# Four reads of transposed tokens moved up by one write in SyncE's queue

## The chip, the cores and the metric

The kernel runs on one core of a Trainium2 chip. The metric is device time in microseconds (us), from the start of the program to its end. An engine executes its own instructions in the order in which the program lists them; engines and transfers tell each other by semaphores.

## What is computed

There are 64 graphs of 256 tokens with 512 channels, in float32, and an adjacency matrix of 256 x 256 for each. Two layers follow each other. Cut to what matters:

```
# layer 0: gated attention, 8 heads of 64 channels
h    = relu(layernorm(x))
q, k, v = h @ Wq.T, h @ Wk.T, h @ Wv.T
attn = softmax(where(adj, q k^T / 8, -inf))        # per head
c    = attn @ v
gate = sigmoid(concat(c, h) @ Wg.T + bg)
x    = x + gate * h + (1 - gate) * c
# layer 1: graph attention, one head
h    = relu(layernorm(x))
Wh   = h @ W
e    = leaky_relu(Wh a1 + (Wh a2)^T, 0.2), masked by adj
x    = x + elu(softmax(e) @ Wh)
```

All matrix products are float32 on TensorE (PE). Each of the larger ones is split into quarters and computed with seven block products instead of eight (Strassen), so it needs sums of input blocks, made on GpSimd (POOL), and sums of partial results, made on VectorE (DVE).

## The kernel before

**Rounds.** The work is software-pipelined. `emit_round(i)` (L650) emits one round, and a round works on four graphs at different stages: graph i (attention), p = i + 1 (its first products and scores), q = i - 1 (gate, then the second layernorm) and r = i - 2, o = i - 3 (graph attention and output). Rounds -1 to 66 are emitted one after the other. The order on every engine is that of the calls, written out by hand; no scheduler changes it.

**Transposes.** Three kinds of matrices must be transposed between stages: the normalized tokens h, the probabilities e, and the gated result y. Apart from the first two graphs and the last ones this is done in three steps: DVE transposes blocks of 32 x 32 (`a_turn`, `turn`, `g_turn`), SyncE (SP) issues a write of the blocks to a scratch tensor in DRAM (`a_send`, `p_send`, `g_send`), and SP issues four reads that bring them back in the other order (`a_fetch`, `p_fetch`, `g_fetch`), each for 32 of the 128 partitions.

**SP's queue.** SP issues nearly all the transfers. It takes them in order; where one has to wait for a semaphore, all that are behind it wait too. From the start of round i the order is

```
p_send(p)      x4   L248  write h of graph p
a_send(i,0,0)  x1   L392  first write of probabilities
a_send(i,0,1)  x1   L392
a_send(i,1,0)  x1   L392  third write
a_send(i,1,1)  x1   L392  fourth write
p_fetch(p)     x4   L255  read h of graph p transposed into hT
a_fetch(i,0,0) x4   L397  read the first probabilities back
g_send(q)      x1   L392  write y
a_fetch(i,0,1) x4   L397
g_fetch(q)     x4   L397  read y back (yT)
a_fetch(i,1,0) x4   L397
g_store(o)     x1   L640  output
g_send_e(r)    x4   L248
load_graph     x2   L92, L93  next x and adj
a_fetch(i,1,1) x4   L397
g_fetch_e(r)   x4   L255
g_send_h(q)    x4   L248,  later g_fetch_h(q) x4 L255
```

A write of probabilities can be issued when `a_turn` (L386, DVE) of its two halves is done. In the program `a_turn(i,1,1,0)`, `g_diff(q)` (POOL, L456), the gate steps "2 c00 4 c10" (PE and DVE/ACT), `g_tanh` (ACT) and `a_turn(i,1,1,1)` stand between the third and the fourth write.

**Semaphores of transfers.** SP's transfers take eight semaphores in turn. In the trace a transfer waits for the one that used the same semaphore eight transfers before, besides its data and its buffer.

**Who uses hT.** The tile `hT` (three buffers) holds the transposed tokens of graph p. `p_sums` (L152 to L155 by way of `token_sums`) makes four sums of its quarters on POOL, S_l. The product of q and k, `p_qk`, starts with step "1", `pma_qk`, which reads hT alone. In PE's order it comes straight after the last step of `g_wh` ("3", `pmc_wh`). Two block columns later PE transposes the edge column of `wh` (`g_edges`, `pe`, L556), and then step "6" of `p_qk`, `pmb_qk`, needs the second sum (L153).

**DVE beside it.** While PE computes `g_wh`, DVE adds up its partial results (L185) and mixes the gate: `g_mix` (L469 and L471, each with two inputs in SBUF), then `g_turn` (L487), whose result `g_send` writes.

Of the kernel before, what the change touches and what calls it, by code (L numbers as in the profile page):

```python
# [22 lines left out]
def kernel(  # L23
# [626 lines left out]
    def emit_round(i):  # L650


        p, q, r, o = i + 1, i - 1, i - 2, i - 3

        def do(fn, g, *args):
            if 0 <= g < B:
                fn(g, *args)
# [37 lines left out]
        do(a_turn, i, 1, 0, 0)  # L695
        do(a_turn, i, 1, 0, 1)
        do(a_send, i, 1, 0)
        do(a_turn, i, 1, 1, 0)
        do(g_diff, q)
        run(g_gate, q, "2 c00 4 c10")  # L700
        do(g_tanh, q, 0)
        do(a_turn, i, 1, 1, 1)
        do(a_send, i, 1, 1)
        do(p_fetch, p)
        do(p_mask, p)
        chore(chores, 2)
        run(g_gate, q, "3 c01")
# [106 lines left out]
    with tc.manual_schedule(engines={getattr(mybir.EngineType, e) for e in ("PE", "SP", "Pool", "DVE", "Activation")}):  # L814
        load_graph(0)
        load_weight("q", nc.sync)
        load_weight("k", nc.scalar)
        load_weight("v", nc.sync)
        p_stats(0, 0)
        p_stats(0, 1)  # L820
        for fn in (p_root, p_bias, p_norm, p_transpose_pe):
            fn(0)
        for i in range(-1, B + 3):
            emit_round(i)
            graphs.pop(i - 3, None)
# [32 lines left out]
```

## Time and profile before

| | |
|---|---|
| device time, median of 3 runs | 3191.97 us (3191.17 to 3193.47) |
| the profiled execution's own time | 3185.72 us |
| its span, first to last instruction | 3183.9 us |
| PE busy | 3125.0 us, 98% of the span |
| DVE, POOL, ACT busy | 2467.8, 1506.3, 1413.6 us |
| SP's transfers, share of 16 DMA engines | 73.9% |
| mean granted clock of PE | 0.994 |

The profiled execution is 6.25 us shorter than the median of the other runs; durations below are its own. The number in front of a line of the timeline is the start in us from the beginning of the span, the next is the length. Idle time is put in brackets with what ended it. A line can join several instructions of one kind (x4), and its length then includes what stands between them.

### The profile page before, as it was taken

Reading aid. Unit: us, or ns where it says so; the run is one execution under the profiler, and the core shown is the slowest. Engines: PE = TensorE matmul, PEld = TensorE weight load, DVE = VectorE, ACT = ScalarE, POOL = GpSimd, SP = SyncE. Lnnn points to the kernel's source line nnn. Section 1 sums busy time; section 2 is a strip of 40 time slices with the busy share of each in tenths; the row PEclk is TensorE's granted clock in tenths of the full one; section 3 lists DMA queues with packets and bytes.
Section 4 is the critical chain, followed back from the end, with each engine's and each line's share of the span. In section 5 each row is a group of like instructions: output and inputs, shape, how many; then the busy total and the mean of one; then the engine's idle time right before and its main releaser. Section 6 shows DMA issues by size and latency. Waiting matters only on the chain.

```text
span 3183.9 us, 66670 instructions
## 1 busy us (share of the span) xinstructions
PE 3125.0 (98%) x22716; PEld 2723.9 (86%) x22716; DVE 2467.8 (78%) x6366; ACT 1413.6 (44%) x3976; POOL 1506.3 (47%) x2183
## 2 busy tenths in 40 slices
PE   7899999999999999999999999999999999999997
PEld 6888888888889888888888898888888888888984
DVE  6777877877877878778778778778787787787774
ACT  2343543543544534435435445445344344454442
POOL 2454544544544545535445445445454454454453
PEclk9999999999999999999999999999999999999998
DMA  5678778777777777787787777777877877877761
GB/s 169 176 173 204 189 180 206 185 180 206 182 190 199 184 191 195 180 203 187 178 211 184 181 207 182 190 197 177 200 189 182 205 186 179 211 183 183 204 170 44
DMA packets 1103394, 590.63 MB, mean 186 GB/s; under 512 B 685776, under 2 KB 1029328, under 8 KB 1103056
## 3 DMA queue, kind: packets, MB, share of 16 engines
q1 hardware_dynamic: 1102000, 585.32, 73.9%
q8 instruction: 182, 2.98, 0.4%
q14 instruction: 156, 1.28, 0.1%
q10 hardware_dynamic: 1056, 1.05, 0.1%
HBM read 304.88 MB, written 281.28 MB: 184 GB/s over the span
## 4 chain that ended last, share of the span: by engine, by line
PE 90%; DVE 4%; POOL 2%; DMA 2%; issue 1%; SPq 1%; ACT 0%; DVEq 0%; POOLq 0%; ACTq 0%
PE pmb_qk L174 11%; PE pmb_z L174 9%; PE pc L418 7%; PE pma_qk L174 7%; PE pmc_qk L174 7%; PE ps L338 6%; PE po L615 6%; PE pma_z L174 6%; PE pmc_z L174 6%; PE pmb_v L174 5%; PE pmb_wh L174 5%; PE pma_v L174 3%; PE pmc_v L174 3%; PE pmc_wh L174 3%; PE pma_wh L174 3%; DVE e L353 1%
## 5 line engine op out<-in xcount | busy, mean ns | idle before, releaser
L362 ACT ACTIVATE e<-e,low 128x256 f32<-128x256 f32 x1024 | 506.5, 499 | 63.3 <-DVE low L353 63.3
L204 POOL TENSOR_TENSOR rs_l<-ve_l,mhalf 128x2 f32<-128x2 f32 x128 | 89.0, 695 | 869.7 <-DVE ve_l L200 869.7
L353 DVE CUSTOM_DVE_ANT_0 e<-ps,mask 128x256 f32<-128x256 f32 x1024 | 362.1, 415 | 100.1 <-PE ps L338 100.1
L377 POOL TENSOR_SCALAR e<-e,rec 128x256 f32<-128x256 f32 x768 | 352.7, 477 | 148.8 <-DVE rec L370 100.4
L386 DVE STREAM_TRANSPOSE eb<-e 128x512 f32<-128x512 f32 x512 | 351.8, 696 | 76.7 <-POOL e L377 63.4
L213 ACT ACTIVATE h_l<-x,nb_l,rs_l 128x512 f32<-128x512 f32 x256 | 194.1, 805 | 212.4 <-DVE nb_l L208 123.5
L152 POOL TENSOR_TENSOR S_l<-hT_l 128x256 f32<-128x256 f32 x128 | 93.4, 730 | 395.9 <-DMA hT_l<-there_h 361.9
L637 POOL TENSOR_TENSOR x<-x,pos 128x512 f32<-128x512 f32 x128 | 160.1, 1272 | 229.3 <-DVE pos L633 229.3
L615 PE MATMUL po<-wh,egT 128*128 128x512 f32 x512 | 242.5, 617 | 2.1 <-ACT egT L598 2.1
L338 PE MATMUL ps<-qk 64*128 64x256 f32 x2048 | 238.9, 383 | 0.6 <-DVE v L185 0.6
L418 PE MATMUL pc<-eT,v 128*64 128x256 f32 x2048 | 235.9, 382 | 0.1
L338 PEld LDWEIGHTS ps<-qk 64*128 64x128 f32 x2048 | 193.1, 187 | 45.3 <-DVE ve_l L200 21.9
L418 PEld LDWEIGHTS pc<-eT,v 128*64 128x64 f32 x2048 | 141.3, 137 | 86.7 <-DMA eT<-there_e 16.3
L239 DVE STREAM_TRANSPOSE h_l<-h_l 128x512 f32<-128x512 f32 x248 | 167.8, 695 | 54.7 <-ACT h_l L213 54.7
L615 PEld LDWEIGHTS po<-wh,egT 128*128 128x128 f32 x512 | 94.3, 194 | 118.5 <-issue 95.1
L362 ACT ACTIVATION_READ_ACCUMULATOR e<-e,low 128x1 f32 x1024 | 194.8, 190 | 0.0
L196 DVE BATCH_NORM_STATS2 bs_l<-x 128x6 f32<-128x512 f32 x256 | 172.9, 675 | 5.4 <-DMA x<-in_x_dram 5.4
L461 ACT ACTIVATE z<-z,hbg 128x256 f32<-128x256 f32 x256 | 116.1, 502 | 105.9 <-DVE z L185 105.9
L456 POOL TENSOR_TENSOR d<-hT_l,cT 128x512 f32<-128x512 f32 x128 | 160.5, 1274 | 0.0
L428 ACT COPY cT<-pc 128x512 f32<-128x512 f32 x128 | 74.9, 585 | 184.5 <-PE pc L418 184.5
L174 PEld LDWEIGHTS pma_z<-hT_l,wgh_sb 128*128 128x128 f32 x1024 | 129.2, 192 | 30.4 <-issue 30.4
L174 PE MATMUL pma_qk<-hT_l,wq_sb 128*128 128x128 f32 x1024 | 139.6, 280 | 11.9 <-DMA hT_l<-there_h 10.1
(146 smaller groups left out, 7964.8 us busy)
## 6 DMA issues: line engine op xcount, KB each, us to landing
there_e<-eb SPq DMA_DIRECT2D x256, 512.0 KB, 3.4
eT<-there_e SPq DMA_DIRECT2D x1024, 128.0 KB, 3.9
there_h<-h_l SPq DMA_DIRECT2D x496, 128.0 KB, 3.3
hT_l<-there_h SPq DMA_DIRECT2D x496, 128.0 KB, 3.3
x<-in_x_dram SPq DMA_DIRECT2D x64, 512.0 KB, 4.0
out_dram<-x SPq DMA_DIRECT2D x64, 512.0 KB, 4.2
there_y<-y SPq DMA_DIRECT2D x62, 512.0 KB, 3.3
yT<-there_y SPq DMA_DIRECT2D x248, 128.0 KB, 3.4
```

What stands on the lines that cost most here:

```text
L174: nc.tensor.matmul(bank[key][(slice(None), *cols)], lhsT, rhs, start=first and i == 0, stop=last and i == len(todo) - 1, skip_group_check= ...
L196: nc.vector.bn_stats(bs, s["x"][:, t, :])
L213: nc.scalar.activation(h[:, t, :], s["x"][:, t, :], AF.Relu, bias=s["nb"][:, t:t + 1], scale=s["rs"][:, t:t + 1])
L239: nc.vector.transpose(h[:, t, :], h[:, t, :])
L338: nc.tensor.matmul(psc[jj, i][:, t, :], qk[r:r + DK, 0, jj, t * P:(t + 1) * P], qk[r:r + DK, 1, jj, :], start=True, stop=True,)
L353: nc.vector.tensor_tensor_reduce(s["e", half, jj][:, i, t, :], s["ps", half][jj, i][:, t, :], s["mask"][:, t, :], -SCALE, HUGE, ALU.add, A ...
L362: nc.scalar.activation(e, e, AF.Exp, bias=s["low", half][:, jj, i, t:t + 1], scale=-1.0, accum_out=s["sums", half][:, jj, i, t:t + 1],)
L377: nc.gpsimd.tensor_scalar(e, e, rec[:, i, t:t + 1], 1.0, ALU.mult, ALU.mult)
L386: nc.vector.transpose(s["eb", half, jj][:, :, 4 * i:4 * i + 4, :].rearrange("p b n c -> p n b c"), e)
L418: nc.tensor.matmul(pc[i * DK:(i + 1) * DK, jj, :].rearrange("p (t a c) -> p t a c", t=NT, c=32), s["v"][:, kc, hd * DK:(hd + 1) * DK], eT[ ...
L456: nc.gpsimd.tensor_tensor(d, s["hT"][:, :, js, :], s["cT"][:, :, js, :], ALU.subtract)
L615: nc.tensor.matmul(pm, s["egT"][:, t, kc, :], s["wh"][:, kc, :, :HH], start=(kc == 0), stop=(kc == NT - 1))
```

## The change

The call `do(p_fetch, p)` moves up by eight lines. Its four reads are now issued behind the third write of probabilities and ahead of the fourth. No instruction is added or removed, and no other engine's order changes: `p_fetch` issues on SP alone. The fourth write comes four transfers later in SP's queue, and the use of the eight semaphores turns with it.

```diff
         do(a_turn, i, 1, 0, 0)
         do(a_turn, i, 1, 0, 1)
         do(a_send, i, 1, 0)
+        do(p_fetch, p)
         do(a_turn, i, 1, 1, 0)
         do(g_diff, q)
         run(g_gate, q, "2 c00 4 c10")
         do(g_tanh, q, 0)
         do(a_turn, i, 1, 1, 1)
         do(a_send, i, 1, 1)
-        do(p_fetch, p)
         do(p_mask, p)
         chore(chores, 2)
         run(g_gate, q, "3 c01")
```

## The prediction

> **What bounds the kernel now.** I read the page from the top: the busy shares, then the groups of instructions with their idle time, then the waits, and last the timeline of a round.
>
> ```profile
> PE 3125.0 (98%) x22716; PEld 2723.9 (86%) x22716; DVE 2467.8 (78%) x6366; ACT 1413.6 (44%) x3976; POOL 1506.3 (47%) x2183
> ...
> L152 POOL TENSOR_TENSOR S_l<-hT_l 128x256 f32<-128x256 f32 x128 | 93.4, 730 | 395.9 <-DMA hT_l<-there_h 361.9
> ...
> L174 PE MATMUL pma_qk<-hT_l,wq_sb 128*128 128x128 f32 x1024 | 139.6, 280 | 11.9 <-DMA hT_l<-there_h 10.1
> ```
>
> PE has 59 us of idle time in all, so no change of order can be worth more than 2%. POOL waits 361.9 us for the tile that the moved reads fill, which looks like much, but POOL is idle half of the time and PE works meanwhile. What counts is the last row: PE itself waited 10.1 us for hT. That is the size of the prize, give or take.
>
> Next, round by round. In an undisturbed round of the timeline the blocks of PE follow each other without a gap:
>
> ```profile
> 1651.03 1.03 PE L174 MATMUL pmc_wh<-w_sb,S_l 128*128 128x257 f32 x4
> ...
> 1651.81 0.73 POOL L152 TENSOR_TENSOR S_l<-hT_l 128x256 f32<-128x256 f32 x1 [6.08 <-DMA hT_l<-there_h]
> ...
> 1651.90 1.05 PE L174 MATMUL pma_qk<-hT_l,wq_sb 128*128 128x128 f32 x8
> ```
>
> The last read landed at 1651.56 (the trace's record of single transfers), POOL started 0.25 us after it, and PE, which needs the same tile, started 0.34 us after it. So hT lands just when PE wants it: such a round takes 48.29 us and loses nothing, but there is no margin. When a transfer is late, PE waits:
>
> ```profile
> 1116.82 1.03 PE L174 MATMUL pmc_wh<-w_sb,S_l 128*128 128x257 f32 x4
> 1118.26 1.13 PE L174 MATMUL pma_qk<-hT_l,wq_sb 128*128 128x128 f32 x8 [0.41 <-DMA hT_l<-there_h]
> ...
> 99.62 2.05 PE L174 MATMUL pma_qk<-hT_l,wq_sb 128*128 128x128 f32 x8 [6.00 <-DMA hT_l<-there_h]
> ```
>
> Here 1.44 us lie between two starts instead of the usual 0.87. The second example is the first round that reads hT through DRAM, still among the start-up work.
>
> **What the Trainium skill says.** "DMA: Bandwidth & Descriptors", Anatomy of one DMA, says that a wait for a semaphore happens on the issuing sequencer and that DMA engines just consume their queues; the section on queues, rings and completion order adds that descriptors are consumed in ring order on each engine. The trace agrees: while the fourth write waits for DVE, SP issues nothing, although hT's source landed 2.4 us (median) before the third write was out. "SBUF — State Buffer", Who interferes with whom, says that a DVE instruction with two inputs in SBUF and a GpSimd instruction that reads SBUF exclude each other. The trace agrees: the output's sum `pos` takes 0.68 us alone and 1.19 us where POOL's sums run beside it, and POOL's L154 takes 1.18 instead of 0.73 us.
>
> **The change, part by part.**
>
> ```profile
> 1645.76 0.32 SPq L392 DMA_DIRECT2D there_e<-eb  x1
> 1646.25 2.61 SPq L255 DMA_DIRECT2D hT_l<-there_h  x4
> 1648.97 1.95 SPq L397 DMA_DIRECT2D eT<-there_e  x4
> ```
>
> *The four reads.* The third write is issued at 1644.02 and takes SP 0.32 us. SP then waits until 1645.76 for the last `a_turn`, issues the fourth write, and starts the reads at 1646.25. With the change they start at 1644.34 + 0.10 = 1644.44, 1.81 us earlier; this is the median over all rounds too. Their data has landed and the buffer is long free, so they bring no new wait. From issue to landing they took 3.3 us just behind a write; the same holds behind the third, so I keep it (2.6 us is the shortest seen for such reads). hT lands at 1651.56 - 1.81 = 1649.75.
>
> *The fourth write.* It is ready at 1645.76, but SP is busy with the reads until 1644.44 + 2.66 = 1647.1: 1.3 us later. Its data is read back by the last `a_fetch` from 1665.49 on, so about 15 us cover a landing of some 3.3 us. Its source buffer is next needed in the following scores, over 25 us later. Cost: nothing.
>
> *What is behind on SP.* The first `a_fetch` moves from 1648.97 to about 1647.5. The waiting time of SP was filled with the reads, so everything behind is earlier or equal, up to `g_send`, which waits for DVE at 1652.34 as before. The eight semaphores: one of the first `a_fetch` reads now waits for the first hT read (landed by about 1647.7, needed at about 1649.0), and the fourth write for a write of h that landed by 1641.8. No wait comes of it.
>
> *PE, steady rounds.* I measured from the last `pmc_wh` matmul to the first `pma_qk` in the 61 rounds from 149 us on. The usual distance is 0.22 us; 17 rounds lie over 0.25, and the excess adds up to 6.8 us, the largest 1.17. All of them are below the 1.81 us gained. After a wait the first block also takes about 0.08 us longer (1.13 for 1.05), in all 1.9 us. Both go: 8.7 us.
>
> *PE, first round.* At 99.62 the shift is 2.5 us, since the fourth write is later there. PE starts at about 97.1, and DVE, 5.6 us idle ahead of the first sum of `p_qk`, can follow: 2.5 us. The matmuls there ran at half clock (2.05 us for 1.05), and whether the clock returns earlier or later is open: plus or minus 1.5 us.
>
> *POOL and DVE, the new collision.* The sums now run from about 1649.95 instead of 1651.81. In an undisturbed round DVE's second L471 starts at 1650.30, with two inputs in SBUF; today POOL is idle then. It must wait for L152 to end at about 1650.68 and needs some 0.54 us more (as `pos` does), so it ends at about 1651.2 instead of 1650.98: 0.2 us, at worst 0.5 as seen on `pos`. L487 and two L185 follow, and their last result is needed by `pe` on PE. From its end to `pe` there are 0.72 us, of which some 0.15 are the weight load and the signal; 0.55 us of cover. Cost: nothing, up to small change in odd rounds. `g_send` may be 0.2 us later, but the reads queued in front of y are gone earlier.
>
> *What is late next.* The last probabilities: the matmul that first needs them starts 1.0 us (median) after they land, at worst 0.14 us. I allow 0.7 us for rounds that meet this instead.
>
> Sum: 6.8 + 1.9 + 2.5 - 0.7 = 10.5 us. The profiled execution would fall from 3185.7 to 3175.2. The runs' median stands 6.3 us above that execution, and I apply the same difference to it: 3191.97 - 10.5 = 3181.5. Bounds of the cost: from 3 us (only the larger waits go, and half comes back at the next one) to 17 us (if the 6.3 us that the runs have over the profile are also late hT, which no view here shows).
>
> **The rivals.**
>
> *It is hidden anyway.* Late rounds might owe their delay to something that moves with PE, so that the next wait, the last probabilities (0.14 us at worst), takes most of it back. For it: 44 of 61 rounds lose nothing today. Against it: that wait costs about 1 us in all rounds together. The gain would be 0 to 6 us: 3186 to 3192, within what can be told.
>
> *Slower, through the lock between POOL and DVE.* If L471 loses twice, to L152 and to L153, it ends about 1.1 us late, against 0.55 us of cover; PE then stalls 0.55 us in each of about 60 rounds: 33 us, 3225 us. It decides from 0.55 us of delay on. For it: L208, 0.15 us long alone, takes 0.72 beside POOL's sums, so the delays are real and can reach 0.57. Against it: on `pos` DVE got its turn after one instruction of POOL in all 60 rounds.
>
> *The change doesn't do what it says.* The reads could be held at the new place, if h's write were late. It landed at least 0.47 us before the third write was issued, in every round. This is part of the first rival.
>
> **How the numbers follow.** Forecast (gain 6.5 to 17 us) 0.70, hidden 0.22, slower by the lock or another way 0.08. About 0.2%, 6.4 us, is what a measurement can tell from no change, so these are also the chances of faster, within, slower. The range 3174 to 3190 holds the forecast from its largest gain and most of the hidden case; the slower tail is left out.
>
> **What would show it.** Right: PE's wait for hT falls from 10.1 us to below 4, nearly all of it in the first round; POOL's L152 waits about 1.8 us less per round (361.9 to about 250); L255 is issued in front of the last `there_e`; L471 takes about 0.9 us in most rounds. Wrong: `pe` or `pmb_qk` waits for DVE's `wh` for more than 10 us, or waits for eT grow by as much as those for hT fall, or hT's time to landing rises by more than 1 us.

## The result and the profile after

| | median, us | runs |
|---|---|---|
| before | 3191.57 (3190.14 to 3193.47) | 6 |
| changed | 3178.28 (3176.11 to 3178.95) | 6 |

The changed kernel is 13.3 us faster: ratio 0.9957, 95% interval 0.9945 to 0.9970. The forecast was 3181.5 us. In two more comparisons the ratio was 0.9947 (0.9935 to 0.9960) and 0.9948 (0.9936 to 0.9961). The profiled execution took 3178.95 us, its span 3177.2 us.

The page of the changed kernel, and the group of the first `p_qk` block from its list of groups:

```profile
PE 3122.1 (98%) x22716; PEld 2726.9 (86%) x22716; DVE 2481.4 (78%) x6366; ACT 1414.0 (45%) x3976; POOL 1528.5 (48%) x2183
...
L152 POOL TENSOR_TENSOR S_l<-hT_l 128x256 f32<-128x256 f32 x128 | 95.2, 744 | 276.6 <-DMA hT_l<-there_h 240.0
```
```profile
L174 PE MATMUL pma_qk<-hT_l,wq_sb 128*128 128x128 f32 x1024 | 137.7, 278 | 5.0 <-DMA hT_l<-there_h 3.6 <-DVE hT_l L143 1.4
```

PE's wait for hT fell from 10.1 to 3.6 us, and those 3.6 us are one wait, in the first round that reads hT (6.00 us before). POOL's wait fell by 122 us, nearly all of it time in which PE was at work.

SP's queue of the changed kernel, in a round of the middle:

```profile
1638.67 0.32 SPq L392 DMA_DIRECT2D there_e<-eb  x1
1639.17 2.60 SPq L255 DMA_DIRECT2D hT_l<-there_h  x4
1641.82 0.60 SPq L392 DMA_DIRECT2D there_e<-eb  x1
```

The reads follow the third write 0.50 us after its issue and fill the time in which SP used to wait for DVE. hT now lands 2.15 us ahead of PE's start of `pma_qk` (median) instead of 0.29 us. The timeline of the same round, POOL, DVE and PE:

```profile
1644.55 0.73 POOL L152 TENSOR_TENSOR S_l<-hT_l 128x256 f32<-128x256 f32 x1 [4.17 <-DMA hT_l<-there_h]
...
1644.93 0.89 DVE L471 SCALAR_TENSOR_TENSOR z<-d,cT 128x512 f32<-128x512 f32 x1
...
1645.35 1.06 POOL L153 TENSOR_TENSOR S_l<-S_l,hT_l 128x256 f32<-128x256 f32 x1
...
1646.53 1.05 PE L174 MATMUL pma_qk<-hT_l,wq_sb 128*128 128x128 f32 x8
...
1648.31 0.38 PE L556 MATMUL pe<-ident,wh 128*128 128x128 f32 x2
```

In the undisturbed round of the kernel before that the prediction shows, the same two instructions were

```profile
1650.30 0.68 DVE L471 SCALAR_TENSOR_TENSOR z<-d,cT 128x512 f32<-128x512 f32 x1
...
1652.61 0.73 POOL L153 TENSOR_TENSOR S_l<-S_l,hT_l 128x256 f32<-128x256 f32 x1
```

The collision is there: L471 takes 0.89 us instead of 0.68, L153 1.06 instead of 0.73. PE's `pe` starts on time. What is late instead, elsewhere in the same execution, is the last part of the probabilities. In the worst round PE waits almost 1 us in the middle of `pc`:

```profile
456.32 2.81 PE L418 MATMUL pc<-eT,v 128*64 128x256 f32 x24
460.08 1.08 PE L418 MATMUL pc<-eT,v 128*64 128x256 f32 x8 [0.95 <-DMA eT<-there_e]
```

Below, the rounds from 149 us on, in which PE's blocks have one order, are called steady: `p_qk` starts 61 times there, with 60 whole rounds between. "Excess" is what a round, or a stretch of it between two blocks of PE, takes over its usual (tenth percentile) length, summed over the rounds; it includes what a restart costs after a wait. The "lateness of hT" is the excess from the start of the last `wh` matmul to the first of `pma_qk`, as in the prediction, and the "eT excess" is that of the stretch of `pc`.

### The profile page after: what moved, and what is told of

Read it like the earlier page. It is cut to its first block, busy times and chain, and to the rows that moved or that the text cites. A ratio compares the mean times of both kernels' runs of the same rounds, so it can differ in the third digit from the quotient of the medians.

```text
span 3177.2 us, 66671 instructions
## 1 busy us (share of the span) xinstructions
PE 3122.1 (98%) x22716; PEld 2726.9 (86%) x22716; DVE 2481.4 (78%) x6366; ACT 1414.0 (45%) x3976; POOL 1528.5 (48%) x2183
## 4 chain that ended last, share of the span: by engine, by line
PE 94%; DMA 2%; DVE 2%; issue 1%; POOL 1%; SPq 0%; ACT 0%; POOLq 0%; DVEq 0%; ACTq 0%
PE pmb_z L174 11%; PE pmb_qk L174 10%; PE po L615 7%; PE ps L338 7%; PE pma_z L174 7%; PE pmc_z L174 7%; PE pc L418 7%; PE pma_qk L174 7%; PE pmc_qk L174 7%; PE pmb_wh L174 5%; PE pmb_v L174 5%; PE pmc_wh L174 3%; PE pma_wh L174 3%; PE pma_v L174 3%; PE pmc_v L174 3%; DMA eT<-there_e 1%
## 5 line engine op out<-in xcount | busy, mean ns | idle before, releaser
L187 ACT COPY qk<-pma_qk 128x512 f32<-128x512 f32 x64 | 37.5, 585 | 245.5 <-PE pma_qk L174 245.5
```

## The experiments

**Theory.** The loss was PE waiting for late hT; margin above the largest lateness is worth nothing. **Rivals.** The gain comes from SP's queue as a whole (every later read comes earlier), or it is small and the profile caught a good execution. Kernels of one comparison ran on one chip, beside the kernel before.

**1. The kernel before, profiled again, twice.** No edit.

> The kernel before, for a second profile: the first one was 6.3 us shorter than the median of its runs. Theory (the runs have more late hT than the profile caught): an execution near 3192 to 3195 us shows 12 to 15 us of excess at the step from wh to pma_qk in the 60 steady rounds and the start-up together, instead of 6.8 and 6.2. Rival (the difference lies in the start-up or in the clock): the steady rounds show 10 to 11 us as before, and the difference is found elsewhere.

> The same once more, with the same expectations, so that two executions stand beside the first profile.

The executions took 3193.03 and 3189.32 us. From the waits of the first:

```profile
POOL S_l L152 <- DMA hT_l<-there_h: 346.4, 55, 8.2
PE pma_qk L174 <- DMA hT_l<-there_h: 12.1, 11, 5.8
```

In the 60 steady rounds all excess together is 15.0 and 14.1 us, against 10.5 us in the first profile. The lateness of hT alone is 10.0 and 8.5 us, against 6.8. So the first profile did catch a good execution: of the 7.3 us between it and the execution of 3193.03 us, 4.6 lie in the steady rounds, 3.2 of them late hT, and 2.0 at the end of the program. With the first round's wait (5.8 and 5.4 us) the lateness is 15.8 and 13.9 us; but the first profile, with 6.8 and 6.0, lay in the expected 12 to 15 us as well, so that this range decides nothing.

The lateness is not spread by chance alone. In seven rounds, those that start `p_qk` of graphs 23, 24, 28, 43, 44, 45 and 59, hT is over 0.2 us late in all three profiles, and these seven hold 4.1 to 4.4 us of it.

**2. Later instead of earlier.** In the kernel before, the reads go behind the first `a_fetch`.

```diff
-        do(p_fetch, p)          # as in the kernel before: behind the fourth write
 ...
         do(a_fetch, i, 0, 0)
+        do(p_fetch, p)
```

> The four hT reads are issued behind the four reads of a_fetch(i,0,0), about 2 us later than in the kernel before, while the first a_fetch itself comes 2.7 us earlier than in the kernel before. Theory: in the kernel before hT landed about 0.2 us ahead of PE's need, so PE now waits about 1.8 us in each of 61 rounds, plus 0.08 us of restart: 110 to 118 us more than the kernel before, about 3305 us. Rival (the gain came from the earlier first a_fetch, or from SP's queue as a whole, not from hT): no slower than the kernel before, 3180 to 3192 us.

One execution: 3372.78 us, 177.6 us above the median of 3195.18 beside it. Waits, and two rounds of PE:

```profile
PE pma_qk L174 <- DMA hT_l<-there_h: 153.4, 62, 8.0
```
```profile
209.35 1.13 PE L174 MATMUL pma_qk<-hT_l,wq_sb 128*128 128x128 f32 x8 [2.31 <-DMA hT_l<-there_h]
260.46 2.04 PE L174 MATMUL pma_qk<-hT_l,wq_sb 128*128 128x128 f32 x8 [2.58 <-DMA hT_l<-there_h]
```

Every round waits, although the first `a_fetch` came 2.7 us earlier than in the kernel before: the rival falls. The size was underestimated twice. Behind the four reads of the first `a_fetch` an hT read takes 3.8 to 3.9 us to land instead of 3.3 to 3.4 (medians), and it is issued 2.1 to 2.2 us later instead of 2, so the wait is 2.5 us a round, not 1.8. And in 15 of the steady rounds the first block runs wholly or mostly at half clock (1.77 to 2.05 us for 1.13); in the trace's clock record there are 18 half-clock stretches of 3.4 us or more in the steady rounds, 68 us long, and the mean granted clock is 0.983 instead of 0.994.

The clock record also shows which gaps cost clock. All half-clock stretches of this trace begin on one grid of 3.41 us. In the steady rounds one begins behind each of 18 grid steps in which PE was idle for 1.98 us or more, and behind none with up to 1.96 us (one step with 2.00 us was not followed either). So a gap of 2 to 3 us costs clock where it falls mostly into one step, and costs none where it is split over two.

**3. Earlier still.** In the changed kernel, the reads go in front of the third write.

```diff
+        do(p_fetch, p)
         do(a_send, i, 1, 0)
-        do(p_fetch, p)
```

> The hT reads are issued in front of the third write too, about 2.4 us earlier than in the changed kernel. Theory: with 2 us of margin PE's waits for hT are gone, further margin is worth nothing: within 2 us of the changed kernel (3176 to 3180). Rival (earlier is always better): 3170 or less. Second rival (lock between POOL's sums and DVE): the sums now meet both L471 and the second L469, each up to 0.5 us longer, and PE stalls at pe or at a product of wh: 5 to 40 us slower than the changed kernel.

> The changed kernel once more, beside the three variants. Theory (late hT at PE was the loss): 13 us less than the kernel before, PE waits under 4 us for hT, all of it in the first round that reads hT, and some 3 to 5 us for the last probabilities (eT). Rival (the profile caught a good execution): PE waits for hT come back in some of the 61 steady rounds.

3182.53 us against 3179.19 for the changed kernel beside it, 3.3 us slower; the intervals of the two ratios (0.9948 to 0.9973 and 0.9935 to 0.9960) overlap, though each of its five runs is longer than each of the five beside it. hT lands 4.6 us ahead of PE instead of 2.15, and that gains nothing. The first rival (earlier is always better) falls, and the theory's "within 2 us" is missed by little. In the profiles the round that follows the first hT read takes 51.4 instead of 48.8 us, since PE there waits 0.87 and 1.82 us for DVE's sums of `p_qk` (why these are late stays open); the steady rounds lose 6.0 instead of 4.9 us. One of the steady rounds shows the second rival's mechanism:

```profile
1694.61 0.73 POOL L152 TENSOR_TENSOR S_l<-hT_l 128x256 f32<-128x256 f32 x1 [1.26 <-DMA hT_l<-there_h]
1694.63 1.26 DVE L471 SCALAR_TENSOR_TENSOR z<-d,cT 128x512 f32<-128x512 f32 x1
...
1695.82 0.41 DVE L185 TENSOR_TENSOR u_wh<-pmb_wh,u_wh 128x257 f32<-128x257 f32 x1
...
1696.38 1.11 PE L174 MATMUL pmb_wh<-w_t,S_l 128*128 128x257 f32 x4 [0.24 <-DVE u_wh L185]
```

POOL starts 20 ns before DVE's L471, DVE loses the turn, the sum of `wh` behind it is late, and PE waits 0.24 us. It happens in six rounds, 1.9 us of excess together, so the mechanism is real, and the 5 to 40 us of the second rival are not reached. The changed kernel beside it is 16.0 us under the kernel before, where 13 were expected. In its profile PE waits 3.5 us for hT, all in the first round, as expected, and the eT excess is 4.0 us.

**4. Half of it.** In the changed kernel, two of the four reads stay in front of the fourth write and two go behind it.

```diff
         do(a_send, i, 1, 0)
         do(p_fetch, p)           # now j = 0, 1 alone
 ...
         do(a_send, i, 1, 1)
+        do(p_fetch_rest, p)      # j = 2, 3
```

> Two of the four hT reads in front of the fourth write, two behind it. The fourth write then goes out when DVE is done, and the last two reads about 1.5 us earlier than in the kernel before. Theory (PE waits only where the last of the four lands over 1 us late, at most 1.17 us in the first profile): nearly the whole gain, within 2 us of the changed kernel, and at least 10 us under the kernel before. Rival (all four must be in front, since the fourth write's 512 KB stand ahead of the rest in the DMA engines): half the gain or less, 3184 to 3190 us on the scale of the first comparison.

SP's queue in a round of the middle (the write of L392 stands in L397 here):

```profile
1640.32 0.32 SPq L397 DMA_DIRECT2D there_e<-eb  x1
1640.83 1.26 SPq L255 DMA_DIRECT2D hT_l<-there_h  x2
1642.13 0.64 SPq L397 DMA_DIRECT2D there_e<-eb  x1
1642.81 1.51 SPq L255 DMA_DIRECT2D hT_l<-there_h  x2
```

3181.34 us, 14.0 under the kernel before beside it (3195.32), ratio 0.9959 (0.9946 to 0.9973). Nearly the whole gain, with little margin: the last read is issued 1.15 us earlier than in the kernel before (median), but takes 4.13 us to land instead of 3.35. It lands only 0.39 us earlier, and in 7 rounds hT is still late, 1.5 us in all. So the rival's delay is real, at 0.8 us, and its conclusion is not: a shift of 0.4 us in the median takes most of the lateness away.

That the fourth write goes ahead does not explain the delay by itself, since in the kernel before it goes ahead of all four reads. But there the DMA engines are only 18% busy in the half microsecond before its data starts to move (mean over 55 rounds), as SP stood waiting for DVE. Here the first two reads are on their way and the engines 99% busy: the write takes 3.78 us to land instead of 3.04, and the reads behind it are late with it.

**5. The next wait.** `a_fetch(i,1,1)` goes in front of `load_graph`, which waits for the write of the output (50.4 us in all in the changed kernel), once in the changed kernel and once in the kernel before.

```diff
+        do(a_fetch, i, 1, 1)
         do(load_graph, p + 1)
 ...
-        do(a_fetch, i, 1, 1)
```

> The changed kernel, and a_fetch(i,1,1) issued in front of load_graph(p+1) instead of behind it. Theory (the waits that are left are for the last probabilities, 3.7 us in the changed profile, because those reads queue behind the load of x, which waits for the output's write): the reads are issued 1 to 2 us earlier, PE's waits for eT fall below 1 us, 3173 to 3176 us. Rival (the DMA engines are full there, landing takes 6.7 us whatever the order): the same as the changed kernel within 1.5 us. Second rival: x comes 2 us later and the layernorm of the next graph becomes late: slower by 5 us or more.

> Not the kernel before but the changed one with a_fetch(i,1,1) in front of load_graph, a second profile: the waits for eT stay below 1 us in the steady rounds, 3175 to 3178 us.

> The changed kernel on the chip of this comparison: 13 to 16 us under the kernel before.

> The changed kernel with a_fetch(i,1,1) in front of load_graph, beside it once more. Theory: steady rounds lose about 2 us instead of 5 to 6 us, so 2 to 4 us under the changed kernel. Rival: no difference that a measurement shows, within 1 us.

> The kernel before, with the hT reads where they were and a_fetch(i,1,1) in front of load_graph(p+1). Theory (in the kernel before nearly all loss at PE in steady rounds is late hT): the waits for eT go, which were about 1 to 2 us, the waits for hT stay at 7 to 10 us: 0 to 3 us under the kernel before. Rival (the order of SP's queue as a whole matters, any read issued earlier helps): 5 us or more under it.

The reads are issued 2.0 us earlier relative to PE, and the last has landed 5.4 us after the first issue instead of 6.7; the matmul that needs them starts 4.1 us after they land instead of 0.8. The eT excess falls from 4.0 us to under 0.1. The group of `pc` in the kernel before, in the changed kernel, and then in this one:

```profile
L418 PE MATMUL pc<-eT,v 128*64 128x256 f32 x2048 | 235.9, 382 | 0.1
```
```profile
L418 PE MATMUL pc<-eT,v 128*64 128x256 f32 x2048 | 237.2, 383 | 2.5 <-DMA eT<-there_e 2.2
```
```profile
L418 PE MATMUL pc<-eT,v 128*64 128x256 f32 x2048 | 235.1, 382 | 0.0
```

| one comparison, medians in us | hT reads as before | hT reads moved |
|---|---|---|
| last `a_fetch` as before | 3194.78 | 3178.87 |
| last `a_fetch` in front of `load_graph` | 3191.74 | 3175.79 |

The moved `a_fetch` is worth 3.0 us alone (ratio 0.9989, 0.9981 to 0.9997) and 3.1 us on top of the changed kernel; in these medians the two changes add up. With both the ratio is 0.9940 (0.9927 to 0.9954). In the comparison before, the same kernel had 3177.12 us against 3179.19, 1.1 us above the 3173 to 3176 that were expected; its second profile took 3177.01 us. The intervals of this kernel and of the changed one overlap, so the advantage of 2 to 3 us is likely, supported by the profiles, and not clear of the noise by itself. With the `a_fetch` alone moved, hT still costs: PE waits 10.7 us for it, and the lateness in the steady rounds is 9.1 us. The rival (any read that comes earlier helps) falls.

## Why the prediction was right

- *The reads start 1.81 us earlier.* Right to 0.1 us: relative to PE they start 1.73 us earlier. From the end of a write to the first read SP takes 0.18 us, as it did behind the fourth write in the prediction's own lines (1646.08 to 1646.25), and not the 0.10 that was used. The last read takes 3.23 us to land instead of 3.35, so hT lands 1.86 us earlier. In the earliest round h's write had landed only 0.16 us before the third write was issued, not 0.47; no reads were held by it.
- *Steady rounds.* Right: the 6.8 us of lateness are all gone, and of the 1.9 us of longer first blocks 0.04 are left. These lay on 29 rounds, so 32 rounds lost nothing before, not 44.
- *First round.* Right: the wait fell by 2.36 us (2.5 forecast). The block after it still ran at half clock, but the half-clock stretch there lasted 3.4 us instead of 6.8, and the next `pma_qk` starts 2.7 us earlier (146.52 instead of 149.25).
- *The fourth write.* Right: it is issued 1.40 us later (1.3), and nothing waits for it.
- *The lock between POOL and DVE.* Right in mechanism and size: the second L471 of a round takes 0.89 us in the median, 0.2 more, and at most 0.56 more (0.5 forecast). From `wh` to `pe` 0.51 us are left of 0.73, at least 0.16, and `pe` never waits in a steady round. How near that is shows in experiment 3.
- *What is behind on SP.* Wrong in part, at a small cost. The prediction held everything behind the reads to be earlier or equal, and gave the 0.2 us of `g_send` no cost. `g_send` is issued 0.21 us later relative to PE, and the last `a_fetch` behind it 0.14 us later: 7.55 us ahead of the matmul that needs it instead of 7.69, and alike in the other profiles (7.53 and 7.56, instead of 7.70 and 7.68). With two reads in front (experiment 4), where L471 takes its usual 0.68 us, `g_send` is not later and the last `a_fetch` stands at 7.66.
- *What is late next.* Right in its place, too small in size: 0.7 us were allowed; the eT excess rose by 3.7 us in the first pair of profiles (0.9 to 4.6). The other profiles have 1.4 and 1.6 us before, 4.0 and 1.6 us after, so that part of the 3.7 is chance.
- *The sum.* The first pair of profiled executions differs by 6.8 us, not 10.5. Up to the first steady `pma_qk` 2.7 us were gained (2.5 forecast), in the steady rounds 5.0 us (8.7 - 0.7 = 8.0 forecast), and the end of the program lost 0.9 us, where a half-clock stretch lasted 6.8 us instead of 3.4; the three profiles of the kernel before have both lengths there.
- *The step from profile to runs.* The prediction applied one difference, 6.3 us, to both kernels. The three profiled executions of the kernel before lie 6.3, 2.3 and 6.0 us below the median of the runs beside them; those of the changed kernel lie 0.7 us above, 0.3 and 2.4 us below. So the runs of the kernel before seem to lose more than its traces show. Part of that is late hT (1.7 and 3.2 us more in the two later profiles than in the first); where the rest lies is not shown. The forecast was 3.7 us too high for the pair of profiles and left out 6.5 us in the step to the runs. The two errors have opposite signs; that the sum came within 3 us of 13.3 is in part luck.

What stays open is why a transfer lands late. In the eleven rounds of the first profile in which hT was over 0.2 us late, some of its reads took 3.6 to 4.7 us in place of 3.3, and in four of these rounds they were also issued 0.2 to 0.3 us late. That seven such rounds come back in every profile speaks for a cause that the program brings with it; the records do not say which. Why the start and the end of the program differ by 1 to 2 us between executions of one kernel wasn't tried either.

## What to carry to other kernels

An engine that issues transfers in order should not stand waiting for one source while another is ready: look in its queue for a wait with data behind it that has landed already. Judge such a move by what the bounding engine waits for (10.1 us here), not by the largest wait on the page (361.9 us, of an idle engine), and count how many rounds are late and by how much: here margin paid up to the largest lateness, and more of it gained nothing and moved work into other collisions. Then look for the wait that was second, since it may take a part back. And profile more than one execution: one alone showed 6.8 us of lateness where the others had 8.5 and 10.0.

## What the runs showed of the hardware

- Idle gaps of PE of 2.0 to 3.4 us, one a round, were followed by half clock in 18 of the 61 steady rounds of experiment 2; in the other 43, gaps of 1.95 to 2.91 us were not. What told them apart in these rounds is a grid of 3.41 us on which all half-clock stretches of the trace begin: 1.98 us or more of idle time within one step were followed by half clock, up to 1.96 us were not, with one exception at 2.00 us.
- A 128 KB read of hT took 3.3 to 3.4 us to land behind one 512 KB write that met nearly idle DMA engines (18% busy), 4.0 to 4.1 us behind a write that met full ones (experiment 4), and 3.8 to 3.9 us behind a write and 512 KB of other reads (experiment 2).
- POOL's first sum, starting 20 ns ahead of DVE's L471, cost DVE 0.57 us (1.26 instead of 0.69).
